# A hand-written issue order for a mixing and feed-forward pipeline, and its inverse roots on GpSimd

## The chip, the cores and the metric

The kernel runs on one core of a Trainium2 chip. The metric is the device time of one execution in microseconds; three runs of the kernel before took 2719.61, 2736.0 and 2738.72 us, and their median, 2736.0 us, is the time before. A core has five engines, each with a queue of its own that it works off in order: TensorE (PE, matmuls and transposes, results in PSUM), VectorE (DVE), ScalarE (ACT, functions from tables), GpSimd (POOL) and SyncE (SP, which here only issues DMAs). POOL issues DMAs as well.

## The reference, cut to what matters

The program is two transformer-like layers on 4096 tokens of 256 features: a linear-attention layer, a mixture of experts, an RWKV-like mixing layer and a gated feed-forward. The change lies in the last two, which are, for each token x:

```
h   = layernorm(x)                          # plain norm ahead of the layer
k, v, r = split(layernorm(h)*g1+b1 @ W_tm)  # each mixed with the token before it
y   = wkv(decay, first, k, v)               # a recurrence over tokens, in log space
x2  = h + sigmoid(r) * y
xn  = layernorm(x2)*g2+b2
kk  = mix(xn @ W_cm, previous x2)           # 256 -> 1024
rr  = sigmoid(mix(xn, previous x2))
x   = x + x2 + rr * (relu(kk)**2 @ W_cp)    # 1024 -> 256
z   = layernorm(x)
h0  = silu(z @ w1 * s1) * (z @ w2 * s2)     # 256 -> 1024, twice
h1  = gelu(h0 @ h1 * sh1); h2 = gelu(h1 @ h2 * sh2)
out = x + h2 @ w3 * s3
```

The two norms of h follow one another, so that the second inverse root is worked out from the first one and its variance.

## The kernel before, in words

The expert stage and all that comes ahead of it is the same in both kernels. The pipeline works on 16 chunks of 256 tokens (NC, TC), in `mixing` (L881) and `ff_split` (L1202). Four pieces of work are Python generators, which yield between steps: `time_mix` (T, L957: gate and add the expert outputs, norms, transposes, the three products pkvr), `wkv` (W, L1012: the recurrence by scans along the tokens), `channel_mix` (C, L1099: transposes px, norm, products pcm and pcp, transposes py) and `steps` of the feed-forward (L1243: norm, transposes xfT, h0, sh1, sh2, out). In round i the loop at L1179 works on chunk i of T, chunk i-1 of W, chunk i-2 of C, and on the feed-forward of the chunk that C finished, whose second half (sh2 and out) falls into the next round. C of chunk 0 comes last, since its first token needs the last one. The string `PLAN` (L1173) says in which order a round calls the generators; a digit calls the feed-forward, from round 3 or from round 4 on.

What the string gives is not the order on the engines. The layer below the kernel collects the instructions, and a scheduler with a priority and estimated costs sets the order of each engine's queue from their dependencies; it also gives out the buffers of the tile pools. So in the kernel before the queues hold steps of several generators mixed together.

Products in the feed-forward are made in halves: an operand is split into `hi` (rounded to the fp32r format) and `lo` (the remainder), and each weight block is multiplied with both (`product`, L1233; `split`, L1239). The h2 and w3 weights don't stay on the chip: `piece` (L1217) loads a block of 512 KB from POOL's queue, into four buffers in rotation. [...] Expert outputs are fetched by four indirect DMAs for each chunk (`fetch`, L907), from POOL's queue, after T's first step of the chunk before. The wkv helpers `with_last` and `keep` (L1023 to L1029) copy single columns on POOL.

An inverse root is a square root on ACT (L935, L1253) and a reciprocal on DVE. ACT holds one set of function tables at a time; Sqrt, Silu, Gelu, Exp, Ln and Sigmoid here need different sets, and a load is put ahead of an operation whose set isn't there.

Of the kernel before, what the change touches and what calls it, by code (L numbers as in the profile page):

```python
# [51 lines left out]
def mk_seq_kernel(ctx: ExitStack, tc: tile.TileContext, a: dict, out: bass.AP):  # L52
# [821 lines left out]

    def tokens(d, n):
        return d[n * TC : (n + 1) * TC, :].rearrange("(i p) d -> p i d", p=P)
# [4 lines left out]
    def mixing(own, early, turn, done):  # L881
# [41 lines left out]
        def stats(srcs, nm, part):  # L923

            n = len(srcs)
            sb = c2.tile([P, n, 6], F32, tag=f"st_{part}", name=f"{nm}_st")
            mv = c2.tile([P, n, 2], F32, tag=f"mv_{part}", name=f"{nm}_mv")
            for i, x in enumerate(srcs):
                nc.vector.bn_stats(out=sb[:, i, :], in_=x)
                nc.vector.bn_aggr(out=mv[:, i, :], in_=sb[:, i, :])  # L930
            return mv, root(mv[:, :, 1], nm, part)

        def root(var, nm, part):
            sd = c2.tile([P, NI], F32, tag=f"sd_{part}", name=f"{nm}_sd")
            nc.scalar.activation(sd, var, AF.Sqrt, bias=eps5)  # L935
            rs = c2.tile([P, NI], F32, tag=f"rs_{part}", name=f"{nm}_rs")
            nc.vector.reciprocal(rs, sd)
# [10 lines left out]
        def flipped(src, evac, nm):  # L948
            for c in range(2):
# [5 lines left out]
                evac(c, pt)  # L955

        def time_mix(n, z):  # L957
            x = [z["x"][:, i, :] for i in range(NI)]
            for q in range(2):
                for i in range(NI):  # L960
# [4 lines left out]
            mv, rs = stats(x, f"ln2_{n}", "t")  # L965
            yield

            v2 = c2.tile([P, NI], F32, tag="v2", name=f"v2_{n}")
            nc.vector.tensor_tensor(v2, rs, rs, ALU.mult)
            nc.vector.tensor_tensor(v2, v2, mv[:, :, 1], ALU.mult)  # L970
            r2 = root(v2, f"ln3_{n}", "u")
            nc.vector.tensor_tensor(r2, r2, rs, ALU.mult)
            yield
            xa = normed(x, mv, rs, f"xa_{n}")
            xaT = c2.tile([P, 2, TC + 1], F32, tag="xaT", name=f"xaT_{n}")
            flipped(xa, lambda c, pt: nc.scalar.copy(xaT[:, c, 1:], pt), f"xaT_{n}")
# [3 lines left out]
            st["xaT"] = z["xaT"] = xaT  # L980
            yield
            xi = normed(x, mv, r2, f"xi_{n}")
            xiT = c2.tile([P, 2, TC], F32, tag="fT", name=f"xiT_{n}")
            flipped(
                xi,
                lambda c, pt: nc.vector.tensor_scalar(
                    xiT[:, c, :], pt, col("g1", c), col("b1", c), ALU.mult, ALU.add
                ),
                f"xiT_{n}",
            )  # L990
            yield
            z["kvr"] = []
            for j in range(3):
                y = c1.tile([P, 2, TC], F32, tag=f"kvr{j}", name=f"kvr_{n}_{j}")
                for h in range(2):
# [5 lines left out]
                    for c in range(2):  # L1001
# [3 lines left out]
                        )  # L1005
                    nc.vector.scalar_tensor_tensor(  # L1006
                        y[:, h, :], pk, col("tm", 2 * j + h), xm, ALU.mult, ALU.add
                    )
                z["kvr"].append(y)
                yield  # L1010

        def wkv(n, z):  # L1012
# [27 lines left out]
            nc.gpsimd.tensor_tensor(eb, kk, m[:, :, 1:], ALU.subtract)  # L1040
            for h in range(2):
                nc.scalar.activation(ea[:, h, :], ea[:, h, :], AF.Exp, bias=col("wd", h))
# [7 lines left out]
            keep("s", s_)  # L1050
            nc.scalar.preload_act_table_set("natural_log_exp_and_others")
# [4 lines left out]
            yield  # L1056

            d = work("wd", "d", (P, 2, 2, TC))
            for h in range(2):
# [6 lines left out]
                )  # L1066
            e1 = work("we", "e1", (P, 2, 2, TC))
# [31 lines left out]
        def channel_mix(n, z):  # L1099
            x2T = z["x2T"]  # L1100
            px = psb([P, NI, D], f"px2_{n}")
            for i in range(NI):
                for c in range(2):
# [3 lines left out]
                    )  # L1107
            src = [px[:, i, :] for i in range(NI)]
            mv, rs = stats(src, f"ln4_{n}", "c")
            yield  # L1110
            xn = normed(src, mv, rs, f"xc_{n}")
            yield
            xnT = c2.tile([P, 2, TC], F32, tag="fT", name=f"xcT_{n}")
            flipped(
                xn,
                lambda c, pt: nc.vector.tensor_scalar(  # L1116
                    xnT[:, c, :], pt, col("g2", c), col("b2", c), ALU.mult, ALU.add
                ),
                f"xcT_{n}",
            )  # L1120
# [3 lines left out]
            for c in range(2):  # L1124
                nc.scalar.activation(
                    xk[:, c, :], x2T[:, c, :TC], AF.Identity, scale=omk[:, c : c + 1]
                )
                nc.scalar.activation(
                    rr[:, c, :], x2T[:, c, :TC], AF.Identity, scale=omr[:, c : c + 1]
                )  # L1130
# [3 lines left out]
            nc.scalar.activation(rr, rr, AF.Sigmoid)  # L1134
            yield
            k2 = c1.tile([P, NF, TC], F32, tag="k2", name=f"k2_{n}")
            for j in range(NF):
                pk = psb([P, TC], f"pcm_{n}_{j}")
                for c in range(2):
                    nc.tensor.matmul(  # L1140
                        pk, w_cm[:, c, j * P : (j + 1) * P], xnT[:, c, :],
                        start=(c == 0), stop=(c == 1),
                    )
                nc.vector.scalar_tensor_tensor(
                    k2[:, j, :], pk, col("cmk", j % 2), xk[:, j % 2, :], ALU.mult, ALU.add
                )
                nc.scalar.activation(k2[:, j, :], k2[:, j, :], AF.Relu)
                nc.gpsimd.tensor_tensor(k2[:, j, :], k2[:, j, :], k2[:, j, :], ALU.mult)
                if j % 2:
                    yield  # L1150
            y = c1.tile([P, 2, TC], F32, tag="xk", name=f"y_{n}")
            for c in range(2):
# [6 lines left out]
                nc.vector.tensor_tensor(y[:, c, :], pv, rr[:, c, :], ALU.mult)  # L1159
                yield  # L1160
            nc.gpsimd.tensor_tensor(y, y, x2T[:, :, 1:], ALU.add)
            yield
            py = psb([P, NI, D], f"py_{n}")
            for i in range(NI):
                for c in range(2):
                    nc.tensor.transpose(
                        py[:, i, c * P : (c + 1) * P], y[:, c, i * P : (i + 1) * P], ident
                    )
                nc.vector.tensor_tensor(z["x"][:, i, :], py[:, i, :], z["x"][:, i, :], ALU.add)
# [4 lines left out]
            "CTCTW" "11C" "WWC" "1C1C1W" "C1C1W" "1TCWC" "1CTC" "1" "2T2T" + 8 * "2" + "T" + 8 * "2"  # L1174
# [4 lines left out]
        for i in range(NC + 4):  # L1179
# [8 lines left out]
            for what in PLAN:  # L1188
                if what in live:
                    next(live[what], None)  # L1190
                else:
                    turn(i, int(what))
# [9 lines left out]
    def ff_split(own, xs):  # L1202

# [39 lines left out]
        def steps():  # L1243
            for n in [*range(1, NC), 0]:
# [3 lines left out]
                sd = d2.tile([P, NI], F32, tag="sd", name=f"ln5_sd_{n}", bufs=1)  # L1248
# [4 lines left out]
                nc.scalar.activation(sd, mv[:, :, 1], AF.Sqrt, bias=eps5)  # L1253
                yield
                nc.vector.reciprocal(sd, sd)
                for i, x in enumerate(toks):
                    nc.vector.tensor_scalar(
                        xn[:, i, :], x, mv[:, i, 0:1], sd[:, i : i + 1], ALU.subtract, ALU.mult
                    )
                xT = halves("x", [P, 2, TC], f"xf_{n}", 1)  # L1260
                for c in range(2):
                    pt = psa([P, TC], f"xfT_{n}_{c}")
                    for i in range(NI):
# [3 lines left out]
                    nc.scalar.copy(xT[0][:, c, :], pt)  # L1267
                    nc.vector.tensor_tensor(
                        xT[1][:, c, :], pt, xT[0][:, c, :].bitcast(F32), ALU.subtract
                    )  # L1270
                yield
                cur = halves("h", [P, NF, TC], f"h0_{n}")
                for j in range(NF):
                    p1 = psa([P, TC], f"pf1_{n}_{j}")
                    p2 = (psc if j % 2 else psp)([P, TC], f"pf2_{n}_{j}")
                    for pp, nm in ((p1, "w1r"), (p2, "w2r")):
                        for c in range(2):
                            product(pp, r[nm][:, c, j * P : (j + 1) * P], xT, c, 2)
                    sl = d2.tile([P, TC], F32, tag="sl", name=f"sl_{n}_{j}")
                    nc.scalar.activation(sl, p1, AF.Silu, scale=col("s1", j))  # L1280
                    if j % 2 == 0:
                        h = d2.tile([P, 2, TC], F32, tag="hf", name=f"hf0_{n}_{j}")
                    nc.vector.scalar_tensor_tensor(
                        h[:, j % 2, :], p2, col("s2", j), sl, ALU.mult, ALU.mult
                    )
                    if j % 2:
                        split(cur, slice(j - 1, j + 1), h, nc.gpsimd)
                    yield
                part = []
                for nm in ("sh1", "sh2"):  # L1290
                    new = halves("h", [P, NF, TC], f"{nm}_{n}")
                    for j in range(NF):
                        if nm == "sh1" and j in (1, 3, 5, 7):
                            part.append(piece(n, len(part)))
                        pp = psa([P, TC], f"p{nm}_{n}_{j}")
                        for k in range(NF):
                            w = r["h1r"][:, k, j * P : (j + 1) * P] if nm == "sh1" else part[j][:, k, :]
                            product(pp, w, cur, k, NF)
# [190 lines left out]
```

## Time and profile before

| | |
|---|---|
| median of three runs | 2736.0 us |
| the profiled execution | 2726.17 us |
| its span in the trace | 2724.6 us |
| busy: PE, DVE, ACT, POOL | 2424.0, 1276.4, 1191.9, 714.5 us |
| mean granted PE clock | 0.887 of full |
| last expert products on PE | 1360.3 us after the start |
| output stores, first to last | 1567.5 to 2719.5 us, 81.6 to 82.2 us apart up to 2304.9 |

A page of the profile has the busy time of each engine, groups of instructions by line and tile with their count, busy time, mean duration and the idle time ahead of them with who ended it, and the chain of work that ended last. A line such as L1235 is a line of the kernel; psh, pcm and the like are the names of tiles. A busy PE is not PE at its peak, as matmuls are pipelined. Windows of time can be asked for, with the busy time of each engine in them.

### The profile page before, as it was taken

What the parts mean: (1) busy time and instruction counts of PE and PEld (TensorE: products, weight loads), DVE (VectorE), ACT (ScalarE), POOL (GpSimd) and SP (SyncE); (2) the same over time, 40 slices, a digit from 0 to 9 for tenths busy, and PEclk for the clock granted to TensorE, in tenths of its full rate; (3) what the DMA queues carried; (4) which work ended last, traced back from release to release, by engine and by line L of the source; (5) the groups of instructions that cost most, each with busy time, mean ns of one, the idle gap of its engine ahead of it and who ended that gap; (6) DMA issues with size and microseconds to landing.
All of it is one profiled execution on the core that took longest, in us unless ns stands there. A gap on an engine that the chain in (4) does not pass through costs nothing.

```text
span 2724.6 us, 36149 instructions
## 1 busy us (share of the span) xinstructions
PE 2424.0 (89%) x13495; PEld 2085.6 (77%) x13495; DVE 1276.4 (47%) x3032; ACT 1191.9 (44%) x2169; POOL 714.5 (26%) x882
## 2 busy tenths in 40 slices
PE   7988999999859999999936988889888889999998
PEld 5766777777748888888824877878877878888887
DVE  5453545454421111110168666656566556666443
ACT  4344434343222222222256566655566555565332
POOL 0137210111010000000055443344443344434221
PEclk9877877787769999999967989989989989999999
DMA  9413100000056556556360442554342554353454
GB/s 375 205 63 101 39 24 9 24 16 24 18 181 221 181 191 203 186 181 202 108 188 16 63 77 47 93 93 86 70 77 48 93 93 86 66 77 62 87 91 78
DMA packets 263496, 282.25 MB, mean 104 GB/s; under 512 B 16976, under 2 KB 238032, under 8 KB 259216
## 3 DMA queue, kind: packets, MB, share of 16 engines
q0 software_dynamic: 160864, 117.20, 21.8%
q1 hardware_dynamic: 102448, 162.65, 17.4%
q8 instruction: 109, 1.79, 0.3%
q14 instruction: 75, 0.61, 0.1%
HBM read 219.26 MB, written 60.56 MB: 103 GB/s over the span
## 4 chain that ended last, share of the span: by engine, by line
PE 22%; DVE 10%; POOL 7%; issue 4%; DMA 4%; ACT 3%; POOLq 0%; DVEq 0%; ACTq 0%
PE psh L1235 11%; PE pcp L1155 4%; PE pf L1235 3%; DMA out_dram<-ot 3%; PE pcm L1140 2%; POOL yg L918 2%; DVE den L1091 2%; DVE aa L1082 1%; DVE sh_lo L1241 1%; POOL d L1078 1%; POOL part L1225 1%; DMA yg<-ys_d,yi 1%; POOL ot L1318 1%; POOL e L1089 1%; DVE xt L962 1%
## 5 line engine op out<-in xcount | busy, mean ns | idle before, releaser
L836 ACT ACTIVATE hT<-peh,b 128x256 f32<-128x256 f32 x312 | 147.9, 474 | 401.4 <-PE peh L832 401.4
L1235 PE MATMUL psh<-sh_hi,part 128*128 128x256 f32 x1024 | 275.9, 305 | 26.6 <-DVE sh_hi L1240 18.7
L1235 PE MATMUL psh<-sh_lo,part 128*128 128x256 f32 x1024 | 273.0, 302 | 11.1 <-DVE sh_lo L1241 10.4
L846 PE MATMUL peo<-w,hT 128*128 128x256 f32 x1248 | 281.9, 379 | 0.0
L832 PE MATMUL peh<-xgT,w 128*128 128x256 f32 x1248 | 280.5, 383 | 0.8 <-DVE xgT L827 0.8
L832 PEld LDWEIGHTS peh<-xgT,w 128*128 128x128 f32 x1248 | 235.2, 191 | 44.8 <-issue 12.8
L850 DVE TENSOR_TENSOR y<-peo,b 128x256 f32<-128x256 f32 x78 | 33.1, 425 | 496.3 <-PE peo L846 417.3
L846 PEld LDWEIGHTS peo<-w,hT 128*128 128x128 f32 x1248 | 234.2, 190 | 30.3
L1235 PE MATMUL psh<-h_hi,h1r 128*128 128x256 f32 x1024 | 250.6, 287 | 1.3 <-POOL h_hi L1240 0.5
L1235 PE MATMUL psh<-h_lo,h1r 128*128 128x256 f32 x1024 | 244.0, 283 | 0.0
L1235 PEld LDWEIGHTS psh<-sh_hi,part 128*128 128x128 f32 x1024 | 209.8, 206 | 34.9 <-DVE sh_hi L1240 22.7
L1303 ACT ACTIVATE hf_sh<-psh,vec 128x256 f32<-128x256 f32 x256 | 117.5, 474 | 253.9 <-PE psh L1235 199.1
L1235 PEld LDWEIGHTS psh<-sh_lo,part 128*128 128x128 f32 x1024 | 211.4, 207 | 17.4 <-DVE sh_lo L1241 15.9
L1235 PEld LDWEIGHTS psh<-h_hi,h1r 128*128 128x128 f32 x1024 | 190.6, 188 | 5.5 <-POOL h_hi L1240 4.1
L1235 PEld LDWEIGHTS psh<-h_lo,h1r 128*128 128x128 f32 x1024 | 191.3, 189 | 0.8
L645 POOL DMA_INDIRECT xe_d<-xr,placei x64 | 63.2, 987 | 448.6 <-DVE placei L640 408.2
L1240 DVE CAST sh_hi<-hf_sh 128x512 fp32r<-128x512 f32 x128 | 66.7, 528 | 219.4 <-ACT hf_sh L1303 219.4
L805 POOL DMA_DIRECT2D xg<-xe_d x39 | 27.8, 712 | 484.4 <-PE pxg L823 454.5
L1225 POOL DMA_DIRECT2D part<-in_h2T_dram x128 | 117.6, 919 | 140.8 <-PE psh L1235 110.5
L404 PE MATMUL pA<-AR,B 128*128 128x256 f32 x512 | 141.9, 401 | 11.5 <-ACT B L422 7.6
L1140 PE MATMUL pcm<-xcT,w_cm 128*128 128x256 f32 x512 | 132.4, 395 | 5.5 <-DVE xcT L1116 5.2
L1003 PE MATMUL pkvr<-xiT,w_tm 128*128 128x256 f32 x384 | 101.2, 422 | 28.4 <-DVE kvr L1006 26.4
(358 smaller groups left out, 5347.1 us busy)
## 6 DMA issues: line engine op xcount, KB each, us to landing
w<-in_w_dram SPq DMA_DIRECT2D x78, 1024.0 KB, 8.8
part<-in_h2T_dram POOLq DMA_DIRECT2D x128, 512.0 KB, 5.5
xe_d<-zero SPq DMA_DIRECT2D x32, 1024.0 KB, 20.1
part<-in_w3T_dram POOLq DMA_DIRECT2D x32, 512.0 KB, 5.0
xg<-xe_d POOLq DMA_DIRECT2D x39, 256.0 KB, 6.8
ys_d<-y SPq DMA_DIRECT2D x39, 256.0 KB, 6.9
b<-in_b_dram SPq DMA_DIRECT2D x39, 128.0 KB, 7.6
x<-in_x_dram SPq DMA_DIRECT2D x8, 512.0 KB, 6.7
```

Of the source, the lines that this page charges most:

```text
L404: nc.tensor.matmul(pA[:, f].rearrange("p g t -> p (g t)"), B[:, f, :], AR[:, f].rearrange("p g t -> p (g t)"), start=True, stop=True,)
L645: nc.gpsimd.indirect_dma_start(out=xe_d, out_offset=bass.IndirectOffsetOnAxis(ap=placei[:, q, t : t + 1], axis=0), in_=xn[:, i, :], in_off ...
L832: nc.tensor.matmul(ph, w1[:, c, h * P : (h + 1) * P], xT[:, c, :], start=(c == 0), stop=(c == 1),)
L836: nc.scalar.activation(hT[:, h, :], ph, AF.Gelu_apprx_tanh, bias=b1[:, h : h + 1])
L846: nc.tensor.matmul(px, hT[:, h, i * P : (i + 1) * P], w2[:, h, :], start=(h == 0), stop=(h == NF - 1),)
L1003: nc.tensor.matmul(pk, w_tm[:, c, o : o + P], xiT[:, c, :], start=(c == 0), stop=(c == 1))
L1140: nc.tensor.matmul(pk, w_cm[:, c, j * P : (j + 1) * P], xnT[:, c, :], start=(c == 0), stop=(c == 1),)
L1155: nc.tensor.matmul(pv, w_cp[:, j, c * P : (c + 1) * P], k2[:, j, :], start=(j == 0), stop=(j == NF - 1),)
L1225: nc.gpsimd.dma_start(out=v, in_=src.rearrange("(c p) n -> p c n", p=P))
L1235: nc.tensor.matmul(pp, w, x[u][:, k, :], start=(k == 0 and u == 0), stop=(k == kk - 1 and u == 1))
L1240: eng.tensor_copy(out[0][:, jj, :], h)
L1303: nc.scalar.activation(h[:, j % 2, :], pp, AF.Gelu, scale=col(nm, j))
```

## The change

The branch is now issued under a manual schedule: each engine gets its instructions in the order of the program. Generators yield at more places, most of all between PE's work and the evacuation of its result. The feed-forward becomes three generators: `norms` (N), `products` (M, PE's work and the part loads) and `results` (E, functions, splits and the output). A capital letter calls them from round 3 on, a small one (the second half of the chunk before) from round 4 on. Inverse roots become an addition and a power on POOL (`root_of`), the small products for the second root go to POOL too. The order of channel_mix's operations changes in places (both rr scalings first, its sigmoid after the second pair of pcm, products in pairs). The split of the last two products of each layer is made one by one on DVE; the output tile has a tag of its own.

```diff
+    mhalf = moe_c.tile([P, NI], F32, name="mhalf")
+    nc.gpsimd.memset(mhalf, -0.5)
+    def root_of(rs, var):
+        nc.gpsimd.tensor_scalar(rs, var, LN_EPS, None, ALU.add)
+        nc.gpsimd.tensor_tensor(rs, rs, mhalf, ALU.pow)
...
         def root(var, nm, part):
-            sd = c2.tile([P, NI], F32, tag=f"sd_{part}", name=f"{nm}_sd")
-            nc.scalar.activation(sd, var, AF.Sqrt, bias=eps5)
             rs = c2.tile([P, NI], F32, tag=f"rs_{part}", name=f"{nm}_rs")
-            nc.vector.reciprocal(rs, sd)
+            root_of(rs, var)
...
-            mv, rs = stats(x, f"ln2_{n}", "t")
-            yield
+            mv = stats(x, f"ln2_{n}", "t")
+            rs = root(mv[:, :, 1], f"ln2_{n}", "t")
             v2 = c2.tile([P, NI], F32, tag="v2", name=f"v2_{n}")
-            nc.vector.tensor_tensor(v2, rs, rs, ALU.mult)
-            nc.vector.tensor_tensor(v2, v2, mv[:, :, 1], ALU.mult)
+            nc.gpsimd.tensor_tensor(v2, rs, rs, ALU.mult)
+            nc.gpsimd.tensor_tensor(v2, v2, mv[:, :, 1], ALU.mult)
             r2 = root(v2, f"ln3_{n}", "u")
-            nc.vector.tensor_tensor(r2, r2, rs, ALU.mult)
+            nc.gpsimd.tensor_tensor(r2, r2, rs, ALU.mult)
             yield
             xa = normed(x, mv, rs, f"xa_{n}")
+            yield
+            pts = flipped(xa, f"xaT_{n}")
+            yield
             xaT = c2.tile([P, 2, TC + 1], F32, tag="xaT", name=f"xaT_{n}")
-            flipped(xa, lambda c, pt: nc.scalar.copy(xaT[:, c, 1:], pt), f"xaT_{n}")
+            for c in range(2):
+                nc.scalar.copy(xaT[:, c, 1:], pts[c])
...
             nc.gpsimd.tensor_tensor(eb, kk, m[:, :, 1:], ALU.subtract)
+            yield
...
+            for jj in range(0, NF, 2):
+                pks = []
+                for j in (jj, jj + 1):
+                    pk = psb([P, TC], f"pcm_{n}_{j}")
...
+                yield
+                for j in (jj, jj + 1):
+                    nc.vector.scalar_tensor_tensor(
+                        k2[:, j, :], pks[j - jj], col("cmk", j % 2), xk[:, j % 2, :],
+                        ALU.mult, ALU.add,
                     )
...
         PLAN = (
-            "CTCTW" "11C" "WWC" "1C1C1W" "C1C1W" "1TCWC" "1CTC" "1" "2T2T" + 8 * "2" + "T" + 8 * "2"
+            "CCTm" "CCme" "WCme" "CWTC" "Cm" "CeW" "Cme" "CWT" "m" "WCT" "Ceme" "CCW" "me" "CTWT"
+            "TTTeT" "CWCC" "mCCme" "NTTTeNT" "NNTT" "MMEMEMEMEMEMEME" "TET" "MMEMEMEMEMEMEMEE"
         )
...
+                        if j >= NF - 2:
+                            split(at[nm], j, h[:, j % 2, :], nc.vector)
+                        elif j % 2:
+                            split(at[nm], slice(j - 1, j + 1), h, nc.gpsimd if nm == "h0" else nc.vector)
+                        yield
...
+                ot = d2.tile([P, NI, D], F32, tag="ot", name=f"ot_{n}", bufs=1)
...
-            def turn(i, u):
-                if i >= 5 - u:
-                    next(steps, None)
-            mixing(own, lambda i, x: early(i, x) if i < 2 else None, turn, xs.__setitem__)
-            for _ in steps:
-                pass
+            def turn(i, what):
+                if i >= (3 if what.isupper() else 4):
+                    next(steps[what.upper()], None)
+            with tc.manual_schedule():
+                mixing(own, lambda i, x: early(i, x) if i < 2 else None, turn, xs.__setitem__)
```

A letter of the new string is one step. T has 18: the gates with stats and roots (1), xa (2), its transposes (3), their copies on ACT and xi (4), its transposes (5), their evacuation (6), then six pairs of a pkvr product and its evacuation. W has eight: m and ea (1), exps (2), s (3), Ln, bb and d (4), min, max, exps and sigmoid (5), den and two products on POOL (6), aa (7), reciprocal and x2 (8). C has 21: px (1), stats (2), norm (3), transposes (4), evacuation (5), scalings on ACT (6), rr (7), then for each pair of pcm the products and their evacuation (8 to 11, 13 to 16, the sigmoid is 12), pcp (17, 18), y (19), py (20), the new x (21).

## The prediction

> **What bounds the kernel now.** I read the page by slices first: from about 1361 us (half the span) the core is in the mixing and feed-forward pipeline, the only part that the change touches. Then I cut that part at the issues of the output stores, one for each chunk (busy time by window; columns: window, its length, then PE, PEld, DVE, ACT, POOL busy, granted clock, DMA share, GB/s):
>
> ```profile
> 1813.40:1895.00 81.60, 72.09 (x465) 66.67 (x464) 50.83 (x106) 47.44 (x77) 33.74 (x44) 0.92 0.41 78
> 1895.00:1976.70 81.70, 72.20 (x466) 66.62 (x465) 50.91 (x106) 47.50 (x77) 33.77 (x45) 0.92 0.42 78
> 2666.30:2719.50 53.20, 46.42 (x356) 45.03 (x356) 18.65 (x34) 14.72 (x28) 9.75 (x14) 0.94 0.47 85
> ```
>
> A steady round takes 81.8 us, and no engine fills it. How much is PE work? The starts of successive matmuls in dense stretches lie 0.120 us apart for a split product, 0.216 for one pass of an fp32 one, 0.109 for a transpose. A round has 352 + 88 + 24 of them (the 464 or so of each window): 42.2 + 19.0 + 2.6 = 63.8 us. So 18 us of a round are waits and half clock. The groups of the pipeline's stretch say where:
>
> ```profile
> L952 PE MATMUL xcT<-ident,xc 128*128 128x128 f32 x64 | 18.5, 393 | 50.8 <-DVE xc L943 50.8
> L1280 ACT ACT_TABLE_LOAD x55 | 70.6, 1283 | 32.5 <-DVE hf L1283 31.8
> L1303 ACT ACT_TABLE_LOAD x42 | 53.9, 1283 | 29.1 <-DVE sh_lo L1241 18.9 <-DVE h_lo L1241 5.0 <-PE psh L1235 4.9
> L935 ACT ACT_TABLE_LOAD x41 | 52.6, 1283 | 0.7
> L1078 POOL TENSOR_TENSOR d<-d,kvr 128x512 f32<-128x512 f32 x32 | 47.6, 1502 | 91.0 <-ACT d L1072 91.0
> L918 POOL DMA_INDIRECT yg<-ys_d,yi x54 | 54.9, 1016 | 23.0 <-issue 11.3 <-DVE xt L962 11.1 <-DVE ln_st L929 0.3
> ```
>
> Table loads take 15 a round on ACT, four gathers sit on POOL, and the transposes of xc wait 3.2 us a round for DVE. The chain of waits in one round shows how these lock:
>
> ```profile
> 1906.03 1.03 POOL yg L918
> 1907.07 0.30 issue
> 1907.37 0.99 POOL yg L918
> ...
> 1910.89 0.63 POOL h_hi L1240
> ...
> 1912.15 0.55 DVE xc L943
> ...
> 1912.74 0.69 PE xcT L952 x2
> ```
>
> The gathers hold POOL for 5 us; a cast behind them holds DVE; the norm behind that holds PE. An in-order queue passes its delay on: this decides the new order too.
>
> **The clock.** The windows around that gap show what it costs further:
>
> ```profile
> 1908.45:1911.86 3.41, 0.00 (x0) 1.00 0.36 95
> 1911.86:1915.27 3.41, 2.53 (x12) 0.50 0.05 20
> 1915.27:1918.69 3.42, 3.00 (x12) 0.50 0.00 0
> ```
>
> An empty window is followed by two at half clock. [...]
>
> **What the change removes.** Its built order has 110 table loads in this part, seven in a steady round; before executes 253 from 1369 us on. That is 143 x 1.283 = 183 us of ACT time, 9 us a round over 20. [...] This shortens the opening of the round (silus between roots and exps), where about 11 us are lost now. The wait of xf for the output store (4.7 us in the round at 1895) goes too, since ot has a buffer of its own. PE's 63.8 us stay. DVE sheds three small reciprocals and products a round and takes six casts of single products (j of 6 and 7) in place of three double ones and one on POOL: under 1 us of its 51, on the path only at the end of sh1, where it counts below.
>
> **What it moves.** Every engine now issues in program order, so I set up the ledger of one steady round by hand, from row durations, less the 0.1 us by which successive ACT and DVE operations overlap: gate 0.48, bn_stats 0.42, a norm from PSUM 0.54, pcm evacuation 0.48, scans 0.73 to 1.21, bb 0.69, d 0.47, gelu 0.47, exps 0.63 and 1.06, split 0.53 + 0.78. Time 0 is PE's end of the eighth sh1 product.
>
> A. PE runs px (0.44) and m1 (1.92, the first sh2 product), to 2.4. DVE finishes the last split at 1.45, stats of ln4 2.55, then T's first step ahead of the norm: four gates 1.6, stats 1.1, to 5.3; xc 0.95, to 6.3. Stall A: 4.0.
>
> B. PE: xcT, m2, m3, to 10.6. POOL does T's root chain from 5.4 (seven operations on 128x2 at 0.3, to 7.5), four gathers with their gaps (4 x 1.29, to 12.65), one part load (0.93) and only then the copy of carry m (13.8) that ea needs. Behind ea (1.4 beside eb) DVE evacuates xcT: 16.1. Stall B: 5.5. Queued behind this ea on DVE are the next split and xa; behind POOL's gathers also the loads of the h2 parts, which still land in time (issued at 13 and 16, 5.5 us to land, needed at 21.5 and 24).
>
> C. PE: pcm 0 and 1, m4, pcm 2 and 3 (to 21.5), m5, xaT, m6, pcm4, to 26.75. pcm5 takes the PSUM buffer of xaT (a ring of three), which ACT frees in order behind: gelus with a load (22.0), split and pcm evacuations on DVE (24.0), relu, load, Ln (26.4), bb, four d, min (29.3), two exps (31.5), load, two sigmoids, copy: 34.4. Stall C: 7.7.
>
> D. PE: pcm5, m7, pcm 6 and 7, m8, xiT, to 41.6. The products of e with v (2 x 1.5) stand on POOL behind squares, which stand behind the gelus after C; aa (2.4) and its product end at 45.5, xiT is evacuated behind them at 46.4. Stall D: 4.8.
>
> After that: two pkvr, pcp (6.9), the two output products, py, three pkvr, xfT: 63.6, with 1.5 us of small waits; h0 8.6 with the last pkvr, and from there sh1 15.4: 87.6. That is 63.8 of work, 22.0 of stalls and 1.8 of small waits. For the clock I add 0.4: of the half windows after A, B and C most lies inside the next stall; by the rule alone four would add 6.8. The round: 88, against 81.8.
>
> **Unknown costs.** The power on GpSimd is in no row. Nearest are its copies of 128x2 (0.18 to 0.46); I take 0.3. The chain also spares a load, a square root and a reciprocal (1.28 + 0.3 + 0.16), so that below nothing is possible: -1. [...] At 2 us for a power, B grows by 3.4 (two roots stand in it), A by nothing (its root has until 5.3).
>
> **Sum.** Start: now the first h0 product stands at 1496.7, 42 us after its px. In the new order two rounds of W chains (about 34 us each) bring px to 1462, and 57 us of the same ledger without m's follow: +22. To the second h0: 88 against 77.6, +10. The next eleven: 88 against 81.2 on average, +75. The last three without T and W (stall A falls to 1.9, B and D go): 193.5 against 204.3, -11. From there to the end 44 against 47.5, -3. Together +93 us. The profiled execution took 2726.17 (span 2724.6), 9.8 below the median of 2736.0; 2726 + 93 = 2819 for it, and about 2830 at the median. A measurement of this kernel (2719.61 to 2738.72) can tell about 1% from no change.
>
> **Rivals.**
> 1. Stall C doesn't close, as ACT is through with the xaT copies when PE gets to pcm5 (at 26.75 instead of 34.4; that is its point of decision). For it: ACT has 9 loads fewer and no longer loads between silus. Against: Ln, exps and sigmoids stand before the copies and each needs DVE. Its price is 7.7 and two half windows, 3.4: a round of 77, eleven times -4.2 = -46, start +12, tail -14: 2690, faster.
> 2. Contention is less than I took (ea 0.7, aa 0.65 each, gathers without gaps): 6 us less, a round of 82. Start +12, eleven times +0.8, tail -17: 2740, no change. The row of d (1.5 where 1.3 occurs) speaks against it.
> 3. Powers of 2 us and half windows at their full price: 3.4 + 3: a round of 94, 2900.
> 4. The order isn't kept and the change does nothing: the built queues stand in program order, so I leave it out.
>
> **Chances.** Forecast (2780 to 2880) 0.56; rival 1 and what is faster still 0.21; rival 2 0.08; rival 3 0.15. Faster by over 1% 0.21, within 0.08, slower 0.71. The range reaches from 2680 to 2905: it takes in rival 1's own number and rival 3's, and leaves the rounds under 76 and over 94 out. The forecast's own: 2780 to 2880.
>
> **What would show it.** Stores about 88 us apart; PE idle before xcT, the first pcm (behind ea, which waits for POOL), pcm5 (behind ACT's xaT copy) and the first pkvr; some 110 table loads; in the last three rounds less than before. Wrong, if the stores come under 80 us apart: then C or B was hidden. A POOL row for the power over 1 us moves B.

## The result, and the profile after

The changed kernel takes 2893.6 us (median of four runs, 2890.5 to 2898.9), against 2733.6 us before: a ratio of 1.060 (95% interval 1.055 to 1.064). It is 160 us slower. The profiled execution took 2894.9 us, with a span of 2893.3 us.

The expert stage is not the place: the first px of the pipeline stands at 1466.1 us, where the prediction had 1462, and the first h0 at 1524.1. From there the rounds are longer. Here is busy time by window, cut at the output stores as it was for the kernel before (window, length, then PE, PEld, DVE, ACT, POOL busy, granted clock, DMA share, GB/s):

```profile
1799.70:1891.70 92.00, 73.97 (x464) 68.16 (x464) 52.37 (x106) 33.97 (x61) 38.88 (x55) 0.87 0.33 69
1891.70:1984.00 92.30, 73.94 (x464) 68.03 (x464) 52.78 (x106) 33.97 (x61) 38.92 (x55) 0.89 0.33 69
2838.10:2888.30 50.20, 46.31 (x356) 44.44 (x356) 19.91 (x41) 14.59 (x28) 11.98 (x15) 0.97 0.56 112
```

A steady round takes 92.2 us instead of 81.8, with the same 464 PE instructions. ACT has 13 us less to do than before (34.0 instead of 47.5), and nothing came of it: no engine is full. The groups of the page that answer to xcT's of before are now these (line, engine, operation, tiles and shape, count, then busy time, mean ns, and the idle time ahead of the group with who ended it):

```profile
L1159 PE MATMUL pcm<-xcT,w_cm 128*128 128x256 f32 x512 | 163.3, 469 | 150.4 <-ACT xaT L988 79.0
L1014 PE MATMUL pkvr<-xiT,w_tm 128*128 128x256 f32 x384 | 117.2, 455 | 52.9 <-DVE xiT L999 47.5
```

PE stood idle for 150 us ahead of the pcm products. The waits of PE in the pipeline (waiting line, what it waited for, us in total, times, longest) are the four places that the prediction called C, B, A and D:

```profile
PE pcm L1159 <- ACT xaT L988: 79.0, 12, 7.7
PE pcm L1159 <- DVE xcT L1133: 56.0, 12, 8.6
PE xcT L959 <- DVE xc L949: 47.9, 16, 4.4
PE pkvr L1014 <- DVE xiT L999: 47.5, 15, 3.5
```

B has one link more: the xcT that PE waits for stands on DVE behind ea, and ea waits for POOL's copy of m, as the prediction had it:

```profile
DVE ea L1050 <- POOL m L1040: 111.5, 15, 9.2
```

In place of the chain of before, here is what ACT does ahead of C's end in one round (the time order of ACT; start, duration, line, operation, and in brackets the idle time ahead of it with who ended it):

```profile
2037.22 0.72 ACT L1066 ACTIVATE eb<-s,eps 128x512 f32<-128x512 f32 x1
2041.22 1.06 ACT L1083 ACTIVATE e<-e 128x1024 f32<-128x1024 f32 x1 [3.27 <-DVE e L1082]
2042.18 1.04 ACT L1086 ACTIVATE d<-d 128x1024 f32<-128x1024 f32 x1
2043.24 1.28 ACT L1087 ACT_TABLE_LOAD   x1
...
2045.59 0.63 ACT L988 COPY xaT<-xaT 128x256 f32<-128x256 f32 x2
```

xaT's transposes were done on PE some 9 us earlier. ACT was free to copy them during the 3.27 us in which it waited for DVE, but its queue held the two exps, a table load and two sigmoids ahead of the copies. PE's pcm waits for the PSUM buffer that the copy frees, one of three that T and C share (`psb`, L61): 6.6 us here, 79.0 us over the run. That is an order's price: the engine with time to spare waits for the wrong thing.

The windows of the clock around C and D show seven half windows in this round, where a round of before had four (at 0.50 of full, from 1901.62, 1911.86, 1915.27 and 1945.99 on in the round at 1895; six of the seven are in the rows, the seventh lies behind A). It is one of the two long rounds, of 93.9 us, each followed by one of 90.3; most of those of 92 us have six:

```profile
2024.16:2027.57 3.41, 1.06 (x3) 0.88 (x4) 2.23 (x5) 1.35 (x3) 3.35 (x5) 0.50 0.79 154
2027.57:2030.98 3.41, 3.41 (x12) 2.87 (x11) 3.19 (x8) 0.66 (x3) 1.60 (x3) 0.50 1.14 214
...
2037.81:2041.22 3.41, 1.63 (x11) 1.17 (x9) 3.07 (x7) 0.14 (x2) 2.06 (x4) 1.00 0.08 9
2041.22:2044.64 3.42, 0.00 (x0) 0.00 (x0) 1.40 (x3) 3.39 (x4) 0.26 (x1) 1.00 1.09 267
2044.64:2048.05 3.41, 2.06 (x5) 1.70 (x6) 0.00 (x0) 3.38 (x7) 0.00 (x0) 0.50 0.12 31
2048.05:2051.46 3.41, 3.41 (x18) 3.41 (x17) 2.50 (x5) 1.12 (x3) 0.98 (x2) 0.50 0.00 0
2051.46:2054.88 3.42, 3.42 (x24) 3.21 (x23) 2.76 (x3) 0.47 (x1) 3.04 (x3) 1.00 0.00 0
2054.88:2058.29 3.41, 0.79 (x7) 0.47 (x5) 2.84 (x5) 1.97 (x5) 2.53 (x4) 1.00 0.00 0
2058.29:2061.70 3.41, 2.75 (x7) 2.22 (x8) 1.62 (x5) 0.05 (x1) 1.45 (x2) 0.50 0.00 0
2061.70:2065.12 3.42, 3.42 (x10) 2.71 (x9) 2.89 (x4) 0.97 (x2) 0.00 (x0) 0.50 0.00 0
```

At half clock PE is "busy" all through the window at 2017.33 (3.41 us of it) and gets less done: successive split products start 0.21 us apart at 2018 and 0.12 us apart at 2021, where the clock is full again (rows not shown).

Last, the power and the addition ahead of it, as groups of POOL in the pipeline:

```profile
L880 POOL TENSOR_TENSOR ln_rs<-ln_rs,mhalf 128x2 f32<-128x2 f32 x62 | 46.4, 748 | 5.2
L879 POOL TENSOR_SCALAR ln_rs<-ln_mv 128x2 f32<-128x2 f32 x47 | 12.9, 275 | 275.6 <-DVE ln_mv L937 267.7 <-DVE ln_mv L1287 7.9
```

### The profile page after: what moved, and what is told of

Same layout as the page of the kernel before. It is cut to its first block, busy times and chain, and to the rows that moved or that the text cites. A ratio compares the mean times of both kernels' runs of the same rounds, so it can differ in the third digit from the quotient of the medians.

```text
span 2893.3 us, 36137 instructions
## 1 busy us (share of the span) xinstructions
PE 2447.7 (85%) x13495; PEld 2108.6 (73%) x13495; DVE 1289.8 (45%) x3032; ACT 993.0 (34%) x1960; POOL 796.9 (28%) x1059
## 5 line engine op out<-in xcount | busy, mean ns | idle before, releaser
L1267 PE MATMUL psh<-sh_hi,part 128*128 128x256 f32 x1024 | 307.2, 330 | 0.4 <-DMA part<-in_h2T_dram 0.4
L1159 PE MATMUL pcm<-xcT,w_cm 128*128 128x256 f32 x512 | 163.3, 469 | 150.4 <-ACT xaT L988 79.0
L1267 PE MATMUL psh<-sh_lo,part 128*128 128x256 f32 x1024 | 286.2, 310 | 0.0
L832 PEld LDWEIGHTS peh<-xgT,w 128*128 128x128 f32 x1248 | 235.3, 191 | 44.8 <-issue 12.8
L1159 PEld LDWEIGHTS pcm<-xcT,w_cm 128*128 128x128 f32 x512 | 114.2, 237 | 175.9 <-ACT xaT L988 83.9
L1267 PEld LDWEIGHTS psh<-sh_hi,part 128*128 128x128 f32 x1024 | 228.0, 223 | 3.6 <-issue 0.5
L1267 PEld LDWEIGHTS psh<-sh_lo,part 128*128 128x128 f32 x1024 | 227.0, 222 | 3.1
L1272 DVE CAST sh_hi<-hf_sh 128x512 fp32r<-128x512 f32 (+1 forms) x160 | 72.6, 454 | 287.0 <-ACT hf_sh L1367 286.9
L1014 PE MATMUL pkvr<-xiT,w_tm 128*128 128x256 f32 x384 | 117.2, 455 | 52.9 <-DVE xiT L999 47.5
```

Of the source, the lines that this page charges most:

```text
L832: nc.tensor.matmul(ph, w1[:, c, h * P : (h + 1) * P], xT[:, c, :], start=(c == 0), stop=(c == 1),)
L1014: nc.tensor.matmul(pk, w_tm[:, c, o : o + P], xiT[:, c, :], start=(c == 0), stop=(c == 1))
L1159: nc.tensor.matmul(pk, w_cm[:, c, j * P : (j + 1) * P], xnT[:, c, :], start=(c == 0), stop=(c == 1),)
L1267: nc.tensor.matmul(pp, w, x[u][:, k, :], start=(k == 0 and u == 0), stop=(k == kk - 1 and u == 1))
L1272: eng.tensor_copy(out[0][:, jj, :], h)
```

## The experiments

The theory: the hand-written order makes PE wait at four places, and the half clock behind them adds to it; none of the new operations is at fault. Its rivals: the order isn't the cause (the finer steps or the power on GpSimd are), or a fixed order costs as such.

### The same edits in the scheduler's order (e1)

```diff
-            with tc.manual_schedule():
-                mixing(own, lambda i, x: early(i, x) if i < 2 else None, turn, xs.__setitem__)
+            mixing(own, lambda i, x: early(i, x) if i < 2 else None, turn, xs.__setitem__)
```

> The changed kernel with all its edits (finer steps, power roots, new string) but without the manual schedule: the scheduler sets the order of the queues again, as it did before. Theory (the loss comes from the fixed order, through waits that in-order queues pass on): 2640 to 2760 us, rounds of 76 to 82 us, no gap of 4 us before pcm. Rival 1 (the power roots on GpSimd cost the time): still above 2850, with the gaps behind ln_rs. Rival 2 (the finer steps or the moved splits cost it): above 2850 too.

Measured: 2623.6 us, a ratio to the kernel before of 0.961 (0.957 to 0.965). That is 270 us less than the changed kernel, and faster than the theory had it. A round takes 71.3 to 72.3 us:

```profile
1817.70:1890.00 72.30, 66.25 (x467) 62.47 (x466) 53.24 (x107) 37.13 (x63) 38.40 (x56) 0.98 0.43 88
1890.00:1961.30 71.30, 66.76 (x466) 62.88 (x465) 53.10 (x106) 37.13 (x63) 37.68 (x55) 0.98 0.43 89
```

The longest waits of PE left are short ones before xfT, and three before pkvr, in the opening; A to D aren't among them:

```profile
PE xfT L1299 <- DVE xf L1291: 35.8, 16, 2.5
PE pkvr L1014 <- DVE kvr L1018: 21.7, 3, 11.7
```

So the edits themselves are good and the order is what costs. With PE's work at 63.8 us a round by the prediction's count, the scheduler leaves 8 us of it unused.

### The roots (e2, e4, e7)

Each takes one of three orders and changes only the roots. In e2 the changed kernel has its square roots on ACT and reciprocals on DVE again; e7 is e1 with the same edit:

```diff
-            root_of(rs, var)
+            nc.scalar.activation(rs, var, AF.Sqrt, bias=eps5)
+            nc.vector.reciprocal(rs, rs)
... the same in `norms`
```

e4 is the kernel before with the power put in:

```diff
... `mhalf` and `root_of` as in the change
-            sd = c2.tile([P, NI], F32, tag=f"sd_{part}", name=f"{nm}_sd")
-            nc.scalar.activation(sd, var, AF.Sqrt, bias=eps5)
             rs = c2.tile([P, NI], F32, tag=f"rs_{part}", name=f"{nm}_rs")
-            nc.vector.reciprocal(rs, sd)
+            root_of(rs, var)
... the same in `steps`
```

> The changed kernel in its manual order, but with its inverse roots by square root on ACT and reciprocal on DVE again. Theory: not faster than the changed kernel (2890 to 2990 us), since the 49 or more further table loads (1.28 each) and DVE's wait for ACT inside the first step of T make stall A longer by what the shorter POOL chain takes off stall B. Rival 1 (the power at 0.7 to 0.8 us, and the chain of 3.5 us that it makes on POOL, cost the time): 2830 us or less.

> The kernel before, scheduler and all, with only the inverse roots changed to the power on GpSimd. Theory: the loads among the silus get fewer (175 in the build against 255), 80 x 1.28 = 103 us less of ACT time, of which half lies on the path at the opening of the rounds: 2650 to 2735 us. Rival 1 (the power on GpSimd is what makes the changed kernel slow): 2760 us or more.

> The changed kernel's edits in the scheduler's order (as e1), with the roots as the kernel before has them (a square root on ScalarE and a reciprocal on VectorE). Tells how much of e1's gain of 110 us is the roots'. Theory (the finer steps give the scheduler room, the roots only take table loads from ScalarE): 2630 to 2690 us, so that the roots are worth up to some 60 us and the steps the rest. Rival (the roots make the gain): 2700 us or more, near the kernel before.

Measured: e2 2878.8 us (ratio 1.054), 15 us faster than with the power, below the range of the theory. e4 2716.2 us (0.994, 0.992 to 0.997), within it. e7 2651.1 us (0.972, 0.969 to 0.976), within it. So the power gains some 18 us in the scheduler's order of before, some 27 in that of the finer steps, and loses 15 in the hand-written one. In this order, then, a part of the theory fails: one of the new operations costs 15 of the 160 us. In the waits of e2, B shrinks from 56.0 to 13.0 us, as POOL reaches the copy that ea needs sooner, A grows from 47.9 to 74.2, as a root now waits for a table load and for ACT, and C grows by 12.8. The three together lose only 4 us. By the starts of h0, the eleven rounds behind the second h0 are 8 us shorter together and the last three 7.5; what makes the last three shorter was not taken apart. The waits of e2:

```profile
PE pcm L1160 <- ACT xaT L989: 91.8, 12, 7.7
PE xcT L960 <- DVE xc L950: 74.2, 16, 6.5
...
PE pcm L1160 <- DVE xcT L1134: 13.0, 10, 5.2
```

The rest of e1's gain, 78 to 83 us, is thus the other edits (the finer steps, the new string, the moved splits and small products) in an order that the scheduler was left to choose. Which of them makes it was not taken apart, but for the output tile's buffer (e8 below, in the kernel before).

### Stall by stall (e3, e9, e10, e11)

Four kernels take one stall each out of the changed kernel, by order alone. e3 lets ACT copy xaT ahead of W's fifth step (C); e9 issues the gathers behind T's second step (B); e10 evacuates xiT ahead of aa (D); e11 puts channel_mix's norm ahead of T's first step (A).

```diff
 # e3
-            ... "CWT" "m" "WCT" "Ceme" ...
+            ... "CWT" "m" "TWC" "Ceme" ...
 # e9
+            seen = 0
...
+                seen += what == "T"
-                if what == "T" and i + 1 < NC and not zs[i + 1]:
+                if what == "T" and seen == 2 and i + 1 < NC and not zs[i + 1]:
 # e10
-            ... "CCW" "me" "CTWT"
+            ... "CCW" "me" "CTTW"
 # e11
-            "CCTm" "CCme" "WCme" ...
+            "CCCmT" "Cme" "WCme" ...
```

> The changed kernel with one exchange in its string: the step with ACT's copies of xaT stands ahead of the wkv step with the two exps and the sigmoid. Theory: the gap of 6.8 us before pcm5 goes, and nearly all of it comes back before pcm7, whose buffer is that of pcm4: its evacuation stands on DVE behind a split that waits for a gelu behind those exps and sigmoids. Rounds of 90 to 93 us, 2860 to 2900 us. Rival (the copy alone is what holds PE): 6.8 us and a half window less a round, 84 us, about 2770 us.

> The changed kernel with the four gathers issued behind T's second step in place of its first; nothing else. Theory (stall B, 4.4 us a round, is the gathers on POOL ahead of the copy that ea needs, and what comes after starts from B's end): pcm starts some 4 us earlier, and so does all that follows, less what 5 us of gathers now take from other POOL work: round 87 to 90 us, 2820 to 2870 us. Rival (C's end doesn't depend on when pcm begins, so what B gives back C takes): 91.5 us or more, above 2880 us.

> The changed kernel with xiT's evacuation ahead of the sum aa on VectorE (T's sixth step ahead of W's seventh); nothing else. Theory (stall D, 3.5 us a round, stands alone: nothing behind it in the round waits, so it comes back in full, with the 1.3 us of half clock behind it): round 87.5 to 89 us, some 12 rounds of 3.5 to 4.5, 2835 to 2855 us. Rival (aa's products, now later, hold the next round's px or W's last step): 91 us or more, above 2880 us.

> The changed kernel with channel_mix's norm and product ahead of T's first step on VectorE; nothing else. Theory (stall A, 3.3 us, is hidden: B's end is set by T's root chain and the gathers behind it on POOL, which start no earlier for it, but 1 us later): A goes and B grows by as much, round 92 to 93.5 us, 2885 to 2925 us. Rival (every stall counts by itself): 88 us, 2840 us.

Measured: e3 2881.9 us (12 less than the changed kernel), e9 2827.3 (66 less), e10 2860.5 (33 less), e11 2924.5 (31 more). The time is within the theory's range in e3, e9 and e11 (there at its top, with rounds of 93.6 us and more, where 93.5 was the most). In e10 the direction is right, but the time is 5 us above the range.

e3: PE's wait for the xaT copies is gone, and a wait of about the same length stands two products later, for DVE's evacuation of a pcm. This is queued behind a split of sh2, the split waits for a gelu, and the gelu stands on ACT behind the same exps and sigmoids (15.3 of its 96.1 us were there before):

```profile
PE pcm L1159 <- DVE k L1166: 96.1, 14, 8.4
...
PE pcm L1159 <- ACT xaT L988: 1.6, 1, 1.6
```

e9: B falls to 4.9 us in all, and C takes a part of it back (6.6 us a time before, 7.6 now):

```profile
PE pcm L1159 <- ACT xaT L988: 91.7, 12, 7.9
```

e10: D is gone, and PE waits before py instead, for POOL's y:

```profile
PE py L1194 <- POOL y L1189: 27.1, 28, 2.9
```

In the order of POOL there, y stands behind the product of e and v and behind x2T, and POOL idled 5.1 us for the e that DVE now finishes later. Before the edit this wait was 4.5 us in all: 22.6 us over 15 rounds, 1.5 us a round, are most of what the expectation lacked.

e11: A only shrinks, from 47.9 to 30.0 us, where the theory had it go, and B doubles, from 56.0 to 110.2:

```profile
PE pcm L1159 <- DVE xcT L1133: 110.2, 13, 12.3
...
PE xcT L959 <- DVE xc L949: 30.0, 16, 3.0
```

T's first step has to be done before POOL can begin its roots, the gathers and the copy that B waits for. Delay it and B ends later. What is left of A, 1.9 us a round, contains the wait for the norm's own root on POOL (1.16 us in e12 below).

### The stalls at once, by another string (e5)

The order is still written by hand. The copies of xaT, the transposes and the evacuation of xiT go ahead of W's fifth to seventh steps; these and channel_mix's sigmoid follow the last pair of pcm, and the gathers T's second step. W's last step and T's last products move into the feed-forward's products, so that more than the four places changes.

```diff
-                if jj == 2:
+                if jj == 6:
...
-            "CCTm" "CCme" "WCme" "CWTC" "Cm" "CeW" "Cme" "CWT" "m" "WCT" "Ceme" "CCW" "me" "CTWT"
-            "TTTeT" "CWCC" "mCCme" "NTTTeNT" "NNTT" "MMEMEMEMEMEMEME" "TET" "MMEMEMEMEMEMEMEE"
+            "CCTm" "CCme" "CWme" "CWTC" "Cm" "CeW" "Cme" "CWT" "m" "T" "Ceme" "CC" "me" "CTTe" "WCW"
+            "TTTT" "W" "CCC" "mCCme" "NTTTeNT" "NN" "MMEMEMEMEMEMEME" "E" "MMEMEME" "W" "MEME" "TMET" "TMET" "E"
...
+            seen = 0
...
+                seen += what == "T"
-                if what == "T" and i + 1 < NC and not zs[i + 1]:
+                if what == "T" and seen == 2 and i + 1 < NC and not zs[i + 1]:
```

> The changed kernel with another order written by hand; no operation is changed. Theory (the loss is in the four places of the order where the matmuls stand still, and the half clock behind them): the string lets xaT's copies, kvr's transposes, xiT and the sigmoids stand ahead of what made them late (stalls B, C and D, 4.4 + 6.8 + 3.5 us, and most of the half clock behind them, some 5 us), and leaves stall A (3.3 us). Round 70 to 76 us, 2640 to 2700 us in all. Rival (an order fixed on every engine costs as such, wherever its steps stand, since it can't give way to what comes late): other stalls come in their places, round above 82 us, above 2760 us.

Measured: 2680.0 us, a ratio to before of 0.982 (0.978 to 0.986). The theory holds for the time; the rounds, 75.9 to 77.3 us, are at or just above the upper end of its range. A fixed order as such isn't the cost: 214 us of the changed kernel lay in where the steps stood. What the 56 us to the scheduler's order (e1) are made of stays open. A is left, as its order was not touched:

```profile
1800.80:1876.90 76.10, 68.83 (x467) 63.04 (x466) 52.20 (x106) 34.89 (x63) 38.80 (x56) 0.98 0.40 84
1876.90:1954.30 77.40, 70.22 (x466) 64.39 (x465) 51.82 (x106) 34.74 (x63) 38.27 (x56) 0.96 0.40 82
```

```profile
PE xcT L959 <- DVE xc L949: 47.9, 16, 4.4
```

### And A as well (e12)

```diff
-            "CCTm" "CCme" "CWme" ...
+            "CCCmT" "Cme" "CWme" ...
```

> The order of e5 (2680 us, rounds of 76 to 77 us, with stall A left as its one long gap) and the norm of e11 ahead of T's first step. Theory (with B to D gone nothing hides A any more, so it comes back in full with the half clock behind it: 2.5 + 1.5 us): round 72 to 73.5 us, 2610 to 2640 us, beside the 71.3 us and 2623.6 us of the scheduler's order. Rival (B takes it again): 76 us, 2675 us or more.

Measured: 2705.8 us, 26 us slower than e5, with rounds of 78.5 us. The theory falls. The rival's side is right, and the loss is larger than its 76 us; it is not the old stall B, though, but a wait that the edit itself brings. DVE's order in one round shows why:

```profile
1998.02 1.00 DVE L949 TENSOR_SCALAR xc<-px,ln_mv,ln_rs 128x256 f32<-128x256 f32 x2 [1.16 <-POOL ln_rs L880]
1998.93 1.67 DVE L970 SCALAR_TENSOR_TENSOR xt<-yg,gate,xt 128x256 f32<-128x256 f32 x4
...
2006.69 0.69 DVE L1050 TENSOR_TENSOR ea<-m 128x512 f32<-128x512 f32 x1 [2.83 <-POOL m L1040]
```

```profile
2001.76 0.22 POOL L879 TENSOR_SCALAR ln_rs<-ln_mv 128x2 f32<-128x2 f32 x1 [3.78 <-DVE ln_mv L937]
```

The norm needs a root that POOL works out in 1.0 us (0.22 + 0.08 + 0.73). With the norm first, DVE waits 1.16 us for it and starts T's gates after that. Their variance reaches POOL 2.2 us later than in e5 (7.5 us after px instead of 5.3), and POOL, which had been waiting for it, gets to m's copy 2.7 us later (12.2 instead of 9.5). ea, and the evacuations of pcm behind it, wait for that. In e5 the gates fill the time that the root takes. So stall A pays for something: the gates that cause it cover a round trip between two engines, and as long as POOL works out the roots, they are cheaper there than behind the norm.

### Matmuls that fill the stalls (e6)

```diff
+        def fill(k, nm):
+            t = psp([P, TC], nm)
+            for _ in range(k):
+                nc.tensor.matmul(t, w_tm[:, 0, :P], w_tm[:, 0, :TC], start=True, stop=True)
...
+            if 2 <= n <= 13:
+                fill(7, f"fa_{n}")
             pts = flipped(xn, f"xcT_{n}")
...
+                if jj == 0 and 2 <= n <= 13:
+                    fill(9, f"fb_{n}")
...
+                    if j == 5 and 2 <= n <= 13:
+                        fill(15, f"fc_{n}")
...
+                    if j + h == 0 and 4 <= n <= 15:
+                        fill(7, f"fd_{n}")
```

> The changed kernel with 38 matmuls a round added, whose output is used by nothing, in the four stalls of chunks 2 to 13 (4 to 15 for the fourth): 7 ahead of xcT, 9 ahead of the first pcm, 15 ahead of the sixth, 7 ahead of the first pkvr. They are a little shorter than the stalls (38 x 0.43 us or less is 16 us against 18). Theory (stalls cost twice, by standing still and by the half clock that is granted after them): the stalls stay about as long from end to end, but what follows runs at the full clock; the round falls from 92 to 86 to 88 us, the whole to 2820 to 2850 us, in spite of the added work. Rival (the longer durations after the stalls are the matmuls' own, or cost nothing on the path): the same 2885 to 2900 us, or longer by the work added.

Measured: 2865.0 us, 29 less than the changed kernel, with 76 PE instructions more in a round (38 matmuls in two passes each). The direction is the theory's and the size isn't. The fills did their work, as the clock is 1.00 in whole rounds, which are 89.8 us long:

```profile
1891.40:1981.20 89.80, 83.22 (x543) 75.36 (x541) 51.95 (x106) 33.84 (x62) 39.34 (x56) 1.00 0.34 71
1981.20:2071.00 89.80, 83.18 (x543) 75.31 (x541) 51.94 (x106) 33.84 (x62) 39.32 (x56) 1.00 0.34 71
```

So the half clock costs 2.4 us of a round of 92.2, not 4 to 6. Counted from the start of px, A ends at 5.7 us in both, B at 16.2 in both and C at 35.6 (35.7 in the changed kernel). PE ran faster between them and waited the longer, since other engines set when a stall ends. Only behind C (1.0 us of it at D's end) and D (1.3 us up to the end of the round) does the full clock come through.

### The output tile's own buffer (e8)

```diff
# the kernel before, power roots as in e4, and
-                ot = d2.tile([P, NI, D], F32, tag="xn", name=f"ot_{n}", bufs=1)
+                ot = d2.tile([P, NI, D], F32, tag="ot", name=f"ot_{n}", bufs=1)
```

> The kernel before with power roots (as e4, 2716 us), and the output tile under a name of its own, so that the feed-forward's first step no longer waits for the output's transfer to release a shared buffer. Tells whether the gain of the scheduler's order over the kernel before is this one buffer. Theory (it is the finer steps): 2650 to 2715 us, since psh's wait of 6.8 us a round goes in part to another wait. Rival (this buffer alone is the gain): 2600 to 2640 us, as e1.

Measured: 2716.2 us, the same as e4. The wait for the output's transfer goes, and psh waits instead, for DVE:

```profile
PE psh L1240 <- DVE sh_hi L1245: 61.1, 22, 5.7
```

It is not this buffer that makes e1 fast.

## Why the prediction was right, and where its sums were off

The prediction named the four stalls, their releasers and their order, and said slower. All four are there, at these releasers. Its sum was too low: it had about 2830 us, and 2893.6 lies above the forecast's own range of 2780 to 2880. Only the wider range, which took in rival 3's 2900, holds it, and that it does so is luck as much as insight. Time from the start of px, which follows sh1 on PE, to the end of each stall and of the round, in us:

| | A | B | C | D | round |
|---|---|---|---|---|---|
| predicted | 6.3 | 16.1 | 34.4 | 46.4 | 88 |
| changed kernel | 5.7 | 16.2 | 35.7 | 48.7 | 92.2 |
| with the clock kept up (e6) | 5.7 | 16.2 | 35.6 | 47.6 | 89.8 |

**The length of the stalls.** They sum to 17.2 us in the round at 2010 (3.2, 4.2, 6.6, 3.3), where the prediction had 22.0. A is shorter as its norm came 0.6 us sooner, the others mostly because what PE runs before them is slower. (By its own terms the prediction has PE at D at 41.3, not 41.6; the end of D doesn't depend on it.) The table, not this sum, is what to compare.

**The round, 4.2 us too short.** The clock term was mis-sized: 0.4 where it is 2.4 (e6). No run shows the 0.4, an estimate of the author's, or the 6.8 beside it, which is half of four windows of 3.41 us; what the runs showed is the 2.4. The reasoning was right that most of the half windows pass inside the next stall. It left out that behind D no further stall comes in the round: there two pkvr take 3.2 us instead of 1.9 and bear it in full (in the rounds of 93.9 us pcp as well, with 8.0 us instead of 6.7). Another 1.0 us comes between C and D.

The step from A's end to B's is 10.5 us, 0.7 longer, and that it is so close is luck: two errors offset each other. T's root chain on POOL takes 3.5 us, from 5.3 to 8.8, where 2.1 was taken, so that ea starts at 15.0 instead of 13.8. But ea takes 0.7 us and not 1.4, as rival 2 had it, and pcm starts behind the first of the two xcT evacuations.

The step from B's end to C's is 1.1 longer, all of it ahead of the gelus, which end at 23.2 where the ledger had 22.0. On DVE two operations for rr stand between xa and the evacuations of pcm; the ledger names only the split and xa there:

```profile
2028.02 0.98 DVE L949 TENSOR_SCALAR xa<-xt,ln_mv,ln_rs 128x256 f32<-128x256 f32 x2
2028.92 0.86 DVE L1149 SCALAR_TENSOR_TENSOR rr<-xcT,vec,rr 128x256 f32<-128x256 f32 x2
```

They would account for 0.8 of the 1.1; no run takes them away. The rest of the round is 1.0 longer, and A 0.6 shorter: 2.0 + 0.7 + 1.1 + 1.0 - 0.6 = 4.2.

**What lies ahead of a half window.** In the prediction's rows an empty window lies ahead of two of them. The rows above show the clock at 0.50 behind windows that were partly busy too: 0.79 us of 3.41 at 2054.88, and (rows not shown) windows with 1.24 us in stall A and 1.54 us at the start of B. There are six or seven half windows in most rounds; at half of 3.41 us each they would cost 10 to 12 us of work, an estimate; the path lost 2.4 (e6).

**The power.** It takes 0.71 to 0.82 us in most cases and not 0.3, the addition 0.22 to 0.37. The nearest row, a copy of 128x2 at 0.18 to 0.46, was no guide for it. The upper bound of 2 us, an estimate that no run shows, was far too high. Rival 3 (2900 us) rested on it for 3.4 of its 6.4 us a round and gave nearly the right total for a reason that was half wrong: the half windows are there, at 2.4 of the 3 us that it took (no run shows the 3), the slow powers aren't. e2 puts the power's cost in this order at 15 us against the old roots.

**The sum.** In the trace the increments are: start +27.3 (predicted +22), second round +14.8 (+10), eleven rounds +113.3 (+75), the last three +12.0 (-11), the end +1.3 (-3): +169 for +93. The eleven rounds average 91.5 us (the last of them takes 85.1), where 88 was taken: 11 x 3.5 is the 38 that the sum lacks there. The second round (92.4 for 88) adds its 4, and the start 5. The step for the last three rounds failed in kind, not in size. It took B and D to go with T, and C with them; but W is still there in the first of the three, and its exps hold a gelu, the split behind it and so DVE's evacuation of a pcm, for which PE waits 8.4 us: the wait of e3, in another round. That round takes 79.7 us. The last two take 68.3 us each, with waits before xfT and xcT and the half clock behind them, where 64.5 was taken.

**Table loads.** There are 110 of them after 1361 us, seven in a steady round, as counted, at 1.283 us each: behind the load at 2043.24 the sigmoid starts at 2044.53. The two exps at 2041.22 and 2042.18 run behind the Ln at 2037.22 with no load between them. For the kernel before it read 15 in a round, and there are 17; so ACT's busy time fell by 13 us a round and not by 9. The round grew all the same: of the loads left, the one at L1087 (1.28 us, in the rows of ACT above) is on the way to C's end.

**Rivals.** Rival 1 (C doesn't close) is out: C is the largest wait. So is rival 2 (less contention): it was right on ea, but the gathers have their gaps (0.30 us) and the round takes 92, not 82. None of them saw that the same edits would be 4% faster than the kernel before in the scheduler's order.

## What to carry to other kernels

In a hand-written order, a step placed ahead of another on one engine delays what stands behind it there, and a PSUM buffer can carry that to an engine that needs none of its data (here ACT's exps and sigmoids ahead of the xaT copies made PE's pcm wait 6.6 us a time, 79.0 us in all); walk a round on paper, from the end of one wait to the end of the next, before fixing it. A stall taken away by itself can come back at the next place that the same late operation holds (e3: 12 us of 79 gained; e11: a loss) or stay away (e9: 66 us gained where the stall had 56; e10: 33 of 47.5); ask what else the late operation holds, and move the late chain, or all of its victims at once (e5: 214 us). Compare a new order first with the scheduler's order of the same steps: here that was the fastest version of all, 2623.6 us.

## What the runs showed of the hardware that was not expected

**The granted clock beside PE's busy time.** In 390 windows of 3.413 us of the changed kernel (1505 to 2837 us), a window at full clock was followed by a half one if PE was busy for less than 1.5 us of it, and by a full one if it was busy for more than 1.82 us (between them both occur). A half window was followed by a full one if PE was busy for 2.81 us or more, and by another half one at 2.76 us or less. So in this run the full clock went behind every window in which PE stood idle for more than 1.9 us of the 3.41, and was back behind every half one in which it stood idle for 0.6 us or less.

**Half clock was cheap between the stalls.** Six half windows in most rounds, 20 of their 92 us, cost 2.4 us (92.2 against 89.8 in e6), as most of them pass where a later wait would have been the longer for a faster clock. Matmuls that nobody needs, put into the stalls, won 29 us all the same (e6).

**A power on GpSimd** of two elements in each partition takes 0.71 to 0.82 us in most cases in the changed kernel (L880, mean 0.748), 2.7 times the addition ahead of it (L879, 0.275).
